# Layer norms scaled by GpSimd, output stores issued by GpSimd, and new ranks, in a two-layer graph network

## The chip, the cores and the metric

The kernel runs on one core of one Trainium2 chip. The metric is device time of one launch in microseconds (us), the median of several runs. The engines of a core are TensorE (PE in the profile, with its weight loads as PEld), VectorE (DVE), ScalarE (ACT), GpSimd (POOL) and SyncE (SP, which here issues transfers). Each engine works through its own queue in order. A change of about 0.2% is the least that a measurement of this kernel can tell from none.

## The reference

Sixteen batches of 1024 nodes with 128 features share one 0/1 adjacency matrix. Two layers follow one another, each with a residual and a layer norm:

```python
def _layernorm(x, axis=-1, eps=1e-5):
    m = jnp.mean(x, axis=axis, keepdims=True)
    v = jnp.var(x, axis=axis, keepdims=True)
    return (x - m) / jnp.sqrt(v + eps)
# layer 0: graph attention
h = x @ others_weight
e = leaky(u1[:, idx1] + u2[:, idx2])        # u1 = h @ a1, u2 = h @ a2
att = softmax(where(adj > 0, e, NEG_BIG), axis=1)
x = _layernorm(x + (att @ h + x @ self_weight))
# layer 1: gated graph network, 5 steps
for _ in range(5):
    m = adj @ h                              # in_matrix = out_matrix = adj, biases as given
    u3 = h @ u3_w.T + u3_b
    z = sigmoid([m, m] @ w3_w.T + w3_b + u3)
    r = sigmoid([m, m] @ w4_w.T + w4_b + u3)
    hv = tanh([m, m] @ w5_w.T + w5_b + r * h @ u5_w.T + u5_b)
    h = (1 - z) * h + z * hv
out = _layernorm(x + h)
```

## The kernel before

**Tiling.** A batch is 1024 nodes by 128 features, worked in two halves `g` (or `e`) of 512 nodes. Batches go in pairs `q = b // 2`. Inside a gated step h is held transposed (`hT`, features on the partitions); the products with the adjacency need it with nodes on the partitions. For these products a value is split in two fp32r parts, by a ScalarE cast (L603) and a VectorE subtraction (L607), into tiles `blk`; the matmuls are those of `product` (L615). For most pairs and steps the two batches' products are combined into seven instead of eight block products, with sums of operand tiles by VectorE (L1061); the first steps of the first pair and the last three steps of the last pair are taken plainly (`PLAIN`).

**A gated step** (`gates`, L1154). For each half: PE multiplies h by u3 (L1170), ScalarE copies it (L1173), PE adds m's part of the r and z gates (L1180), ScalarE takes their tanh (L1183; sigmoids are taken by tanh of the half), VectorE makes r times h (L1190), PE forms the candidate in two matmuls, the second of which reads r's product (L1196, L1197), ScalarE takes its tanh (L1205), and VectorE updates h in three operations (L1208, L1211, L1214).

**From a step to the next** (`leave`, L1228). VectorE transposes h in 32x32 blocks into a tile `T` (L573), SP writes it to DRAM tile `X` in four transfers of 64 KB (`away`, L583) and reads it back with nodes on the partitions into a tile `G` (`back`, L591). In some places PE transposes instead (L565).

**The two layer norms** (`layernorm`, L516). For each half: VectorE's statistics of four 128x128 chunks (`look`, L521, L523), GpSimd's (variance + eps) to the power -1/2 on 128x4 values (`power`, L527 to L537, with a bias -mean times that for the scale that follows), and the scale: four ScalarE activations with scale and bias (`scale`, L542), or, for the very last halves, four VectorE operations that subtract and multiply (`scale_short`, L548). The first norm (`y`) reads what came back from DRAM into tile `F`; for batches 0 and 1 it reads PSUM. Its result goes to tile `y0`, to DRAM tile `yd` by SP (L991), and on to the second layer. The second norm (`o`) works in an `o` tile, of which there are two: SP loads `yd` into it (L1270), VectorE adds h (L1281), statistics, power and scale follow in place, and SP stores it to the output (L1302, 256 KB a half). Odd batches work with the sign of h turned against the even ones (`sign`), which is why `power` has two forms.

**What sets the order.** All operations are added to a `Plan` (L36) with an engine, a length, a rank, what they read and write, and where needed a lag from their end to a reader's start. `Plan.order` runs through these as a list schedule: of what is ready on an engine, the lowest rank goes first, provided that tiles of its kind are free (`"o": (2, ...)` and so on). What comes out is a fixed order for each engine. The numbers in `D` (L303) are added to the rank of a batch and step, `10 * (b // 2) + 4.2 * s`; `LATER` is added for batch 15 in its plain steps; `LATE` is the lag of the loads in `back`; `IDLE` is a number of filler pairs of PE transposes with the worst rank. The planned lengths and lags only order the work: on the chip every engine waits for what its next instruction reads.

Of the kernel before, what the change touches and what calls it, by code (L numbers as in the profile page):

```python
# [13 lines left out]
ALU = mybir.AluOpType  # L14
AX = mybir.AxisListType

P = 128
# [8 lines left out]
LOW, HIGH = -20.0, 100.0  # L26
TINY = 1e-30
PLAIN = {(0, 0), (0, 1), (0, 2), (7, 2), (7, 3), (7, 4)}
LATER = 1
AHEAD = range(4, 12)  # L30
LATE = 3001
TURNED = {(0, 0), (7, 2), (7, 3)}
IDLE = 100

# [103 lines left out]
def kernel(  # L138
# [51 lines left out]
    nc = tc.nc  # L190
    B = x_t.shape[0]
# [26 lines left out]
    def exact(pools):  # L218
# [80 lines left out]
        def sp(*a, **k):  # L299
            plan.add("SP", *a, **k)  # L300


        D = dict(m=-0.2, pu=1.4, u=0.2, pr=0.2, pz=1.4, r=1.7, pv=1.0, z=0.3, hv=0.2, h=0.8, tr=1.2, o=4.2, ln=3.3)  # L303
        D.update(out=4.0, l1=-9, l2=-3, l3=-3, l4=-4, l5=-4, l6=-3.5, l7=0, l8=-2)

        def on_pe(b, what):

            return b < 2 and what in ("y", "b") or b >= B - 3 and what == STEPS - 1 or (b // 2, what) in TURNED
# [8 lines left out]
        def rank0(b):  # L317
            return 10 * (b // 2) - 1 * (1 - b % 2) + -1.0

        def sign(b):  # L320

            return 1 if b % 2 else -1
# [190 lines left out]
            dve(2 * V, 1 + c / 4, t24, reads=[*y, (("tab",), c, 0)], writes=[(("tab",), c, 1)])  # L513


        def layernorm(key, g, rank, after, src, dst, write, sg=1, short=False):  # L516
            stats, mv, rstd = ("stats", *key, g), ("mv", *key, g), ("rstd", *key, g)

            def look():
                for j in range(4):  # L520
                    nc.vector.bn_stats(T(stats)[:, j, :], src(j))  # L521
                for j in range(4):
                    nc.vector.bn_aggr(T(mv)[:, j, :], T(stats)[:, j, :])  # L523

            def power():
                mean, var, r = T(mv)[:, :, 0], T(mv)[:, :, 1], T(rstd)
                nc.gpsimd.tensor_scalar(r[:, 0, :], var, EPS, None, ALU.add)  # L527
                nc.gpsimd.tensor_tensor(r[:, 0, :], r[:, 0, :], mhalf[:, 0:4], ALU.pow)
                if short:
                    if sg < 0:  # L530
                        nc.gpsimd.tensor_scalar(r[:, 0, :], r[:, 0, :], -1.0, None, ALU.mult)
                elif sg > 0:
                    nc.gpsimd.tensor_scalar(r[:, 1, :], mean, -1.0, None, ALU.mult)
                    nc.gpsimd.tensor_tensor(r[:, 1, :], r[:, 1, :], r[:, 0, :], ALU.mult)
                else:
                    nc.gpsimd.tensor_tensor(r[:, 1, :], mean, r[:, 0, :], ALU.mult)
                    nc.gpsimd.tensor_scalar(r[:, 0, :], r[:, 0, :], -1.0, None, ALU.mult)  # L537

            def scale():
                r = T(rstd)  # L540
                for j in range(4):
                    nc.scalar.activation(  # L542
                        dst(j), src(j), AF.Identity, bias=r[:, 1, j : j + 1], scale=r[:, 0, j : j + 1]
                    )

            def scale_short():
                for j in range(4):
                    nc.vector.tensor_scalar(  # L548
                        dst(j), src(j), T(mv)[:, j, 0:1], T(rstd)[:, 0, j : j + 1], ALU.subtract, ALU.mult
                    )  # L550

            after = after if isinstance(after, list) else [after]
            dve(1100, rank, look, reads=after, writes=[(stats, 0), (mv, 0)])
            plan.add("POOL", 2301 if short else 3001, rank, power, reads=[(mv, 0)], writes=[(rstd, 0)])
            if short:
                dve(900, rank, scale_short, reads=[*after, (mv, 0), (rstd, 0)], writes=[write])
            else:
                act(1250, rank, scale, reads=[*after, (mv, 0), (rstd, 0)], writes=[write])
# [66 lines left out]
        def layer0(b):  # L625
# [323 lines left out]
            for g in range(2):  # L949
                rank = rank0(b) + D["l5"]  # L950

                def y(g=g):
                    return T(yT[g])

                t = ("ps", "t", b, "y", g)
                if on_pe(b, "y"):
                    transposes(y, [(yT[g], 0)], t, rank)
                else:
                    k, d, t = (x + (b, "y", g) for x in (("T",), ("D",), ("F",)))
                    turn(k, y, [(yT[g], 0)], rank)  # L960
                    away(k, d, rank)
                    back(d, t, rank)

                def src(j, t=t, flat=on_pe(b, "y")):
                    return T(t)[:, j * P : (j + 1) * P] if flat else chunks(T(t))[:, j]

                def dst(j, g=g, flat=on_pe(b, "y")):
                    c = T(y0[g])[:, j, :]
                    return c if flat else c.rearrange("p (a j) -> p a j", a=4)

                layernorm(("y", b), g, rank0(b) + D["l6"], (t, 0), src, dst, (y0[g], 0), sign(b))

            if not plain(b // 2, 0):

# [253 lines left out]
        def leave(b, s):  # L1228

            rank = rank_of(b, s)  # L1230
            hT = ("hT", b)
            for g in range(2):

                def h(g=g):
                    return T(hT)[:, g * HALF : (g + 1) * HALF]

                k, d = ("T", b, s, g), ("X", b, s + 1, g)
                if s < STEPS - 1 and on_pe(b, s):
                    t = ("ps", "t", b, s, g)
                    transposes(h, [(hT, g)], t, rank + D["tr"])  # L1240
                    split(
                        ("blk", b, "h", s + 1, g),
                        lambda t=t: T(t).rearrange("p (c a j) -> p c a j", c=4, a=4),
                        [(t, 0)],
                        rank_of(b, s + 1),
                    )
                    continue
                if s < STEPS - 1:
                    turn(k, h, [(hT, g)], rank + D["tr"])
                    away(k, d, rank + D["tr"])  # L1250
                    continue

                t = ("ps", "t", b, s, g)
                n = pieces(b, s)
                done = [(hT, g)] if n == 1 else [(hT, g, i) for i in range(n)]
                if on_pe(b, s):
                    for i in range(n):
                        transposes(h, [done[i]], t, rank + D["tr"], range(4 * i // n, 4 * (i + 1) // n), i)
                else:
                    t = ("F", b, s, g)  # L1260
                    turn(k, h, [(hT, g)], rank + D["tr"])
                    away(k, d, rank + D["tr"])
                    back(d, t, rank + D["o"])


                o, yd = ("y0" if b == B - 1 else "o", b, "o", g), ("yd", b, g)
                sp(
                    450,
                    rank + (D["o"] if b < B - 1 else 0),
                    lambda o=o, yd=yd: nc.sync.dma_start(T(o).rearrange("p c d -> p (c d)"), T(yd)),  # L1270
                    reads=[(yd, 0), (hT, g) if b < B - 1 else (("m", b, s, 0), 0)],
                    writes=[(o, "y")],
                    lag=2300,
                )
                for i in range(n):

                    def last(i=i, t=t, o=o, flat=on_pe(b, s)):
                        cs = slice(4 * i // n, 4 * (i + 1) // n)
                        x = T(o)[:, cs, :].rearrange("p c (a j) -> p c a j", a=4)
                        v = T(t).rearrange("p (c a j) -> p c a j", c=4, a=4) if flat else chunks(T(t))  # L1280
                        nc.vector.tensor_tensor(x, v[:, cs], x, ALU.add)  # L1281

                    dve(V / n, rank + D["o"], last, reads=[(t, i), (o, "y")], writes=[(o, "raw", i)])

                def at(j, o=o):
                    return T(o)[:, j, :]

                layernorm(
                    ("o", b),
                    g,  # L1290
                    rank + D["ln"],
                    [(o, "raw", i) for i in range(n)],
                    at,
                    at,
                    (o, 0),
                    sign(b),
                    b == B - 1 or b == B - 2 and g,
                )
                sp(
                    450,  # L1300
                    rank + D["out"],
                    lambda o=o, g=g: nc.sync.dma_start(  # L1302
                        out[b].rearrange("(c p) d -> p c d", p=P)[:, 4 * g : 4 * g + 4, :], T(o)
                    ),
                    reads=[(o, 0)],
                )


        def look_at(i):
# [336 lines left out]
```

## Time and profile before

| what | before |
| --- | --- |
| median of three runs | 1468.24 us (1467.56 to 1468.84) |
| the profiled execution | 1466.94 us, its span 1465.1 us |
| PE busy | 1444.8 us (99%) |
| VectorE busy | 1170.5 us (80%) |
| ScalarE busy | 896.5 us (61%), of it the scales of L542 47.8 for `o`, 46.0 + 6.0 for `y` |
| GpSimd busy | 157.0 us (11%), of it the power itself (L528) 39.9 + 38.3 |
| mean granted TensorE clock | 0.995 |
| transfers issued | all by SP: 568 writes of transposed h, 144 loads `G`, 30 + 30 `o` loads and output stores, among others |

"Busy" is time in which an engine executes; a wait says that the next instruction of an engine had not got what it reads. A line of a group gives the source line, engine, operation, output and inputs, count, then summed busy time, mean ns of one, and the idle time ahead with what ended it. Overlapping instructions of one engine are counted once in its busy time. `SPq` is SP's queue of transfers: a wait there holds every transfer behind it.

### The profile page before, as it was taken

Reading aid. Unit: us, or ns where it says so; the run is one execution under the profiler, and the core shown is the slowest. Engines: PE = TensorE matmul, PEld = TensorE weight load, DVE = VectorE, ACT = ScalarE, POOL = GpSimd, SP = SyncE. Lnnn points to the kernel's source line nnn. Section 1 sums busy time; section 2 is a strip of 40 time slices with the busy share of each in tenths; the row PEclk is TensorE's granted clock in tenths of the full one; section 3 lists DMA queues with packets and bytes.
Section 4 is the critical chain, followed back from the end, with each engine's and each line's share of the span. In section 5 each row is a group of like instructions: output and inputs, shape, how many; then the busy total and the mean of one; then the engine's idle time right before and its main releaser. Section 6 shows DMA issues by size and latency. Waiting matters only on the chain. (4 is left out here: it accounts for less than half of the span.)

```text
span 1465.1 us, 17965 instructions
## 1 busy us (share of the span) xinstructions
PE 1444.8 (99%) x5084; PEld 907.3 (62%) x5084; DVE 1170.5 (80%) x2777; ACT 896.5 (61%) x1790; POOL 157.0 (11%) x260
## 2 busy tenths in 40 slices
PE   9999999999999999999999999999999999999996
PEld 7767656665666566666666665666666666566563
DVE  6777689878888788987888798996889877866435
ACT  5564665667666666576667676556666666654543
POOL 0101100011100210110201110100201102000101
PEclk9999999999999999999999999999999999999998
DMA  8325724464435553455534543455424444223201
GB/s 300 137 68 156 217 72 137 122 188 130 123 101 155 169 145 84 145 146 153 142 103 128 166 130 93 119 149 165 130 75 128 133 133 117 70 65 87 72 0 32
DMA packets 207233, 182.61 MB, mean 125 GB/s; under 512 B 34751, under 2 KB 154262, under 8 KB 207126
## 3 DMA queue, kind: packets, MB, share of 16 engines
q1 hardware_dynamic: 206562, 180.54, 42.4%
q8 instruction: 42, 0.69, 0.2%
q10 hardware_dynamic: 564, 0.85, 0.2%
q14 instruction: 65, 0.53, 0.1%
HBM read 100.92 MB, written 80.39 MB: 124 GB/s over the span
## 5 line engine op out<-in xcount | busy, mean ns | idle before, releaser
L1197 PE MATMUL ps_g_v<-r,u5h 128*128 128x512 f32 x320 | 163.7, 593 | 2.7 <-DVE r L1190 2.7
L1196 PE MATMUL ps_g_v<-m,wm 128*128 128x512 f32 x320 | 163.4, 592 | 0.0
L1180 PE MATMUL ps_g_r<-m,wm 128*128 128x512 f32 x320 | 160.4, 598 | 0.5 <-ACT gz L1173 0.5
L1180 PE MATMUL gz<-m,wm 128*128 128x512 f32 x320 | 158.8, 592 | 0.0
L1208 DVE TENSOR_TENSOR hv<-hv,hT 128x512 f32<-128x512 f32 (+1 forms) x162 | 109.8, 679 | 56.5 <-ACT hv L1205 56.0
L1170 PE MATMUL ps_g_r<-hT,u 128*128 128x512 f32 x320 | 152.8, 592 | 0.0
L615 PE MATMUL ps_acc_a<-tab,blk_s 128*128 128x512 f32 x544 | 146.8, 412 | 0.1
L1183 ACT ACTIVATE r<-ps_g_r,bh 128x512 f32<-128x512 f32 x160 | 109.1, 686 | 57.5 <-PE ps_g_r L1180 54.9
L1190 DVE SCALAR_TENSOR_TENSOR r<-r,hT 128x512 f32<-128x512 f32 x160 | 108.4, 683 | 42.4 <-ACT r L1183 41.8
L615 PE MATMUL ps_acc_po<-adj,blk 128*128 128x512 f32 x512 | 139.0, 420 | 0.0
L1183 ACT ACTIVATE z<-gz,bh 128x512 f32<-128x512 f32 x160 | 109.7, 687 | 28.0 <-PE gz L1180 27.6
L615 PEld LDWEIGHTS ps_acc_a<-tab,blk_s 128*128 128x128 f32 x544 | 100.9, 188 | 33.1 <-issue 8.0
L615 PEld LDWEIGHTS ps_acc_po<-adj,blk 128*128 128x128 f32 x512 | 96.0, 188 | 35.3 <-issue 10.3
L1173 ACT COPY gz<-ps_g_r 128x512 f32<-128x512 f32 x160 | 91.5, 573 | 42.5 <-PE ps_g_r L1170 40.7
L1197 PEld LDWEIGHTS ps_g_v<-r,u5h 128*128 128x128 f32 x320 | 60.4, 189 | 80.1 <-issue 60.2
L1214 DVE SCALAR_TENSOR_TENSOR hT<-hv,hT 128x512 f32<-128x512 f32 (+1 forms) x162 | 108.0, 670 | 1.7
L1211 DVE SCALAR_TENSOR_TENSOR hv<-z,hv 128x512 f32<-128x512 f32 (+1 forms) x162 | 108.1, 670 | 1.5 <-ACT z L1183 0.4
L1180 PEld LDWEIGHTS gz<-m,wm 128*128 128x128 f32 x320 | 60.7, 190 | 74.3 <-issue 73.8
L573 DVE STREAM_TRANSPOSE T<-hT 128x512 f32<-128x512 f32 x142 | 99.0, 700 | 0.2
L615 PE MATMUL ps_acc<-adj,blk_h 128*128 128x512 f32 x384 | 97.6, 407 | 1.2 <-ACT blk_h L603 0.8
L603 ACT CAST blk_s<-G 128x512 fp32r<-128x512 f32 x136 | 82.9, 617 | 22.0 <-DVE G L1061 19.1
L607 DVE TENSOR_TENSOR blk_s<-G,blk_s 128x512 fp32r<-128x512 f32 x136 | 90.7, 678 | 6.8 <-ACT blk_s L603 6.2
(176 smaller groups left out, 2481.5 us busy)
## 6 DMA issues: line engine op xcount, KB each, us to landing
G<-X SPq DMA_DIRECT2D x144, 256.0 KB
X<-T SPq DMA_DIRECT2D x568, 64.0 KB
yd<-y SPq DMA_DIRECT2D x32, 256.0 KB
xt<-in_x_dram SPq DMA_DIRECT2D x15, 512.0 KB
o_o<-yd SPq DMA_DIRECT2D x30, 256.0 KB
out_dram<-o_o SPq DMA_DIRECT2D x30, 256.0 KB
pb<-ud SPq DMA_DIRECT2D x14, 512.0 KB
D_y<-T_y SPq DMA_DIRECT2D x112, 64.0 KB
```

Source lines behind the costliest of these rows:

```text
L573: nc.vector.transpose(T(t).rearrange("p (b c i) -> p b c i", b=4, c=4), turned(src()))
L615: nc.tensor.matmul(T(bank), T(blk)[:, k, c, :], right(c), start=(first and i == 0), stop=(last and i == len(terms) - 1), skip_group_check= ...
L1170: nc.tensor.matmul(T(pr), u3, h(), start=True, stop=True)
L1173: nc.scalar.copy(T(pz), T(pr))
L1180: nc.tensor.matmul(T(p_), wm[:, j, :], T(m), start=False, stop=True, skip_group_check=True)
L1183: nc.scalar.activation(T(t), T(p_), AF.Tanh, bias=bh[:, j : j + 1], scale=0.5 * sg)
L1190: lambda r=r, h=h: nc.vector.scalar_tensor_tensor(T(r), T(r), 1.0, h(), ALU.add, ALU.mult),
L1196: nc.tensor.matmul(T(pv), wm[:, 2, :], T(m), start=True, stop=False)
L1197: nc.tensor.matmul(T(pv), u5h, T(r), start=False, stop=True)
L1208: nc.vector.tensor_tensor(T(hv)[:, w], T(hv)[:, w], h()[:, w], ALU.subtract)
L1211: nc.vector.scalar_tensor_tensor(T(hv)[:, w], T(z)[:, w], 1.0, T(hv)[:, w], ALU.add, ALU.mult)
L1214: nc.vector.scalar_tensor_tensor(h()[:, w], T(hv)[:, w], 0.5, h()[:, w], ALU.mult, ALU.add)
```

## The change

Three things are changed together. The layer norms' scale goes from ScalarE to GpSimd wherever the values lie in SBUF: `y` of batches 2 to 15 and `o` of batches 0 to 13, 56 halves of four operations each. GpSimd subtracts the mean and multiplies by the power, so that `power` no longer needs the bias: odd batches lose two small operations, even ones lose one and do their sign first. The output stores of batches 0 to 13 are issued by GpSimd, with a planned length of 900 and a lag of 2600 ns to the next use of the tile. The last two batches keep the old scales and SP's stores. And `LATER`, `LATE` and seven of the offsets `D` are set anew.

```diff
-LATER = 1
+LATER = 2.5
-LATE = 3001
+LATE = 3801
-        D = dict(m=-0.2, pu=1.4, u=0.2, pr=0.2, pz=1.4, r=1.7, pv=1.0, z=0.3, hv=0.2, h=0.8, tr=1.2, o=4.2, ln=3.3)
-        D.update(out=4.0, l1=-9, l2=-3, l3=-3, l4=-4, l5=-4, l6=-3.5, l7=0, l8=-2)
+        D = dict(m=-0.2, pu=1.4, u=0.4, pr=0.6, pz=1.4, r=1.9, pv=0.6, z=0.7, hv=0.2, h=0.8, tr=1.2, o=4.2, ln=3.3)
+        D.update(out=3.6, l1=-9, l2=-3, l3=-3, l4=-4, l5=-4, l6=-3.5, l7=0, l8=-1)
...
-        def layernorm(key, g, rank, after, src, dst, write, sg=1, short=False):
+        def layernorm(key, g, rank, after, src, dst, write, sg=1, short=False, own=False):
...
-                if short:
+                if short or own:
...
+            def scale_own():
+                for j in range(4):
+                    nc.gpsimd.tensor_scalar(
+                        dst(j), src(j), T(mv)[:, j, 0:1], T(rstd)[:, 0, j : j + 1], ALU.subtract, ALU.mult
+                    )
...
-            if short:
+            if own:
+                plan.add("POOL", 2001, rank, scale_own, reads=[*after, (mv, 0), (rstd, 0)], writes=[write])
+            elif short:
...
-                layernorm(("y", b), g, rank0(b) + D["l6"], (t, 0), src, dst, (y0[g], 0), sign(b))
+                layernorm(("y", b), g, rank0(b) + D["l6"], (t, 0), src, dst, (y0[g], 0), sign(b), own=not on_pe(b, "y"))
...
                     b == B - 1 or b == B - 2 and g,
-                )
-                sp(
-                    450,
-                    rank + D["out"],
-                    lambda o=o, g=g: nc.sync.dma_start(
-                        out[b].rearrange("(c p) d -> p c d", p=P)[:, 4 * g : 4 * g + 4, :], T(o)
-                    ),
-                    reads=[(o, 0)],
-                )
+                    b < B - 2,
+                )
+
+                def out_(o=o, g=g, by=nc.gpsimd if b < B - 2 else nc.sync):
+                    by.dma_start(out[b].rearrange("(c p) d -> p c d", p=P)[:, 4 * g : 4 * g + 4, :], T(o))
+
+                if b < B - 2:
+                    plan.add("POOL", 900, rank + D["out"], out_, reads=[(o, 0)], writes=[((o, "sent"), 0)], lag=2600)
+                else:
+                    sp(450, rank + D["out"], out_, reads=[(o, 0)])
```

## The prediction

> **What bounds the kernel now.** I read the page's busy times first, then the windows, then the waits of TensorE, then the timeline around each wait. The windows come first here (columns: window, its length, then busy us and count of PE, weight loads, VectorE, ScalarE, GpSimd, then granted clock, DMA share, GB/s):
>
> ```profile
> 0.00:100.00 100.00, 98.66 (x512) 72.17 (x513) 70.38 (x241) 59.45 (x153) 9.23 (x25) 1.00 0.52 179
> 100.00:200.00 100.00, 98.25 (x372) 64.18 (x371) 78.94 (x209) 55.95 (x118) 9.88 (x16) 1.00 0.51 151
> 200.00:500.00 300.00, 300.00 (x1032) 188.66 (x1031) 257.28 (x592) 188.85 (x375) 29.19 (x48) 1.00 0.48 138
> 500.00:600.00 100.00, 97.91 (x326) 59.87 (x324) 89.00 (x203) 64.73 (x129) 11.92 (x16) 0.98 0.43 120
> 600.00:1300.00 700.00, 699.92 (x2344) 432.37 (x2343) 585.60 (x1333) 450.20 (x882) 82.07 (x128) 1.00 0.44 125
> 1300.00:1400.00 100.00, 98.45 (x335) 60.59 (x334) 55.45 (x111) 50.68 (x90) 7.92 (x16) 1.00 0.24 71
> ...
> 1450.00:1465.10 15.10, 1.61 (x10) 0.80 (x8) 9.95 (x47) 1.15 (x3) 4.41 (x7) 0.64 0.24 75
> ```
>
> TensorE (PE) is busy 1444.8 of 1465.1 us. All it lacks is 1.3 at the head, 1.75, 2.1, 0.1, 1.55 in mid-stream and 13.5 in the last 15. "Busy" is modelled at its ends, so I also summed the matmuls at the spacing that they show where nothing waits (0.43 us for an fp32 512-column one, 0.23 for fp32r): 1437 us, of which 22 are fillers, and 15 us of gaps: 1.8 at the start, 2.5 at 172-180, 4.1 at 500-510 (of which some 1.7 is a clock of 0.98), 2.1 at 1370-1378, 2.5 before the last transposes at 1453, and scraps; another 11.3 follow the last matmul. The change leaves PE's instructions the same, so **the most that it can win in mid-stream is about 8.5 us**. What PE waited for (us in all, times, longest):
>
> ```profile
> PE ps_t L565 <- DVE hT L1214: 3.3, 2, 2.3
> PE ps_g_v L1197 <- DVE r L1190: 2.7, 2, 2.1
> ...
> PE ps_acc L615 <- ACT blk_h L603: 0.8, 1, 0.8
> PE ps_g_r L1180 <- ACT gz L1173: 0.5, 1, 0.5
> ```
>
> Behind these stand loads, not ScalarE's load of work. At 500 ScalarE's cast waited 3.73 us for `G<-X`, its r tanh and VectorE's r product stood behind it, and PE waited 2.09 us at 504.47; at 178 a cast waited 3.00 for another `G<-X`:
>
> ```profile
> 178.13 0.62 ACT L603 CAST blk_h<-G 128x512 fp32r<-128x512 f32 x1 [3.00 <-DMA G<-X]
> ...
> 500.29 0.62 ACT L603 CAST blk_x<-G 128x512 fp32r<-128x512 f32 x1 [3.73 <-DMA G<-X]
> ```
>
> At 1370 and 1378 it is an `o` load. VectorE's add (L1281) waited for it 7.8 us, and the load stood in SP's queue behind the store of an earlier batch from the same buffer (waits of VectorE, then of SP's queue: us in all, times, longest):
>
> ```profile
> DVE o_o L1281 <- DMA o_o<-yd: 12.3, 4, 7.8
> ...
> SPq L1302 <- ACT o_o L542: 124.2, 21, 70.6
> ...
> SPq L1270 <- DMA out_dram<-o_o: 22.1, 12, 3.0
> ```
>
> So SP's queue loses 124 us waiting for ScalarE's scale and 22 for stores to land. This queue, and not ScalarE (896.5 us, 61%), is where the change can bring something.
>
> **What the Trainium skill says.** "SBUF — State Buffer", section Who interferes with whom: a VectorE instruction with two SBUF inputs and a GpSimd instruction that reads SBUF exclude each other for a whole instruction. The trace agrees for GpSimd: its 128x4 add took 0.50 us at 254.03 while such a VectorE operation ran, and 0.23 where none did; VectorE's two-input operations took 0.68 either way. From the timeline:
>
> ```profile
> 253.79 0.66 DVE L607 TENSOR_TENSOR blk_s<-G,blk_s 128x512 fp32r<-128x512 f32 x1
> ...
> 254.03 0.50 POOL L527 TENSOR_SCALAR rstd_y<-mv_y 128x4 f32<-128x4 f32 x1 [97.33 <-ACT r L1183]
> ```
>
> "DMA: Bandwidth & Descriptors", section Issuing engines are not separate DMA queues: issuing elsewhere saves only sequencer time; GpSimd's path has a first byte at about 1 us against 0.6 (Specifications). No store here goes by GpSimd, so no run shows it yet.
>
> **The change, part by part.** Base: this execution, 1466.94 us (span 1465.1 and 1.84 around it); the median of the runs shown is 1468.24, 1.30 above.
>
> *Scale off ScalarE.* Its groups:
>
> ```profile
> L542 ACT ACTIVATE o_o<-o_o,rstd_o 128x128 f32<-128x128 f32 x116 | 47.8, 485 | 7.4 <-DVE o_o L1281 3.0 <-DMA X<-T 1.5 <-DVE mv_o L523 1.3
> L542 ACT ACTIVATE y<-F_y,rstd_y 128x128 f32<-128x128 f32 x112 | 46.0, 484 | 1.6 <-POOL rstd_y L534 1.6
> ```
>
> Of the 116, 112 go, and all of the second row's. 224 at 0.485 summed 108 us, some 92 without their overlap; ScalarE falls to about 805. PE never waited for L542, and ScalarE waited at the two stalls for a load: worth 0 by itself; it shortens the queue ahead of later r and z tanh's. If this cover is missing, nothing is lost.
>
> *Scale onto GpSimd.* No row has this operation. Below: the tiny operations' 0.23 us plus 124 more elements at the 1.03 cycles of 1.2 GHz ("GPSIMD Engine Reference", 3.1) = 0.34; GpSimd's only 128x128 operations in the trace, a memset of 0.20 and a select of 0.29, agree. Above: 1.8 cycles and a wait for one VectorE operation, 0.23 + 0.19 + 0.3 = 0.72. I take 0.55, an estimate: 2.2 us per half against ScalarE's 1.65, 123 in all. The power step loses two tiny operations of 0.36-0.55 in odd batches and one of some 0.4 in even ones: about 34 us of GpSimd in all, 0.6 per half. So the chain power-scale is as long as before; GpSimd goes from 157 to some 250, plus 28 stores, below 20%. Behind a scale on GpSimd's queue stand only other halves' powers, scales and stores; the scale waits for nothing but its power, whose statistics came from the same tile. In the changed order both powers come first in some batches (o of 3, 11, 12, 13): there the first half's scale waits for the second half's statistics too, which I count at 1-3 us of delay, with the stores below. Of y, the readers are SP's store of y (it waited 57 us in all for ScalarE's scale) and the transposes for the second layer, tens of us of PE work ahead of their use: 0.
>
> *What it does to VectorE.* 0 to 0.34 us for each of 224 = 0 to 76 us on 1170. At most 1.4 us per half, and four at once only if each hits. Cover: between r's product and the PE operation that reads it 98% of the pairs have 1.25 us or more (median 3.2). I take 0.5 us in all; if VectorE really stood 1.4 us in each half, those in the stretch with VectorE at 89.00 of 100 would show.
>
> *Stores by GpSimd.* 28 issues of about 0.4 leave SP (11 us of SP, which is not full), and with them SP's 124 us of waiting on the scale, nearly all of which stood before other loads and writes. The wait isn't gone: the next `o` load (L1270), still on SP, waits until the store has landed, since there are two `o` buffers. Behind a blocked L1270 stand SP's writes of h (L583) and loads of G and F (L591), and behind those ScalarE's casts. Its price: at present store to next load takes 2.4 us (1356.85 to 1359.23, 1361.02 to 1364.40); with 0.4-1 more for the software path, and in pairs where GpSimd runs two powers and two scales before the first store some 2.5 more. Even to odd reload took 7.5-12.6 us and becomes 8-15. In mid-stream the add has slack; before the last pair's plain steps it did not (the 7.8 above).
>
> *Ranks.* LATE puts the loads of G 0.8 us later in the plan, hence further behind their writes on SP: the waits for `X<-T` (70.4 us over 109) shrink, and the loads behind them run earlier. In the new order the add of batch 13 has 28-30 us of PE work between its inputs and its reader, where it had 20-24: I expect the 1370 and 1378 stalls gone (-2.1, I take -1.8). The q=0 load that stalled at 178 has 18.1 us of PE work for it instead of 16.3: gains 1.8, of a stall of about 1.4 with its second part: -1.4. Around 504 the instructions stand differently and the r product has 3 us: -2.2 (the clock's 1.7 stay). Against it: the last steps' u to r distance falls from 1.34 to 0.86 us in two places, 0.2 each, the shortest v product to next split falls from 18.6 to 15.0 (a load chain takes at least 13.5), and fillers are used up by row 169: +0.5 to +2, I take +1.0. LATER 2.5 lets batch 15 trail 14 by half a step; the end's chain of transposes, add, stats, power, scale and store has the same members (batches 14, 15 keep VectorE's scale and SP): 0 +-1.
>
> Sum: -1.4 - 2.2 - 1.8 + 0.5 + 1.0 = -3.9, so 1463.0 for an execution like the profiled one and **1464.3** for the median.
>
> **Rivals.** *No change (chance 0.23):* every reordering of so full a plan makes other loads late; the three stalls leave and as many of 1-2 us come: 1468.2, 1465.3-1471.2. For it: PE at 99%, and causes that are single late loads. Against: the distances above grew at the places that stalled.
>
> *Slower (0.35):* SP is blocked at the `o` load. If the store lands 3-5 us later than the plan supposes (GpSimd held by VectorE's two-input operations, scale above 0.9 us, both scales before both stores), each odd batch's first `o` load holds SP and the G loads behind it. They have 1.5-5 us over the 13.5 us load chain; it decides once SP is held over some 3 us. A third of 28 loads by 1-2 us of PE wait each: 9 x 1.5 = +13, less the 4 gained: 1477, range 1471.2-1485. For it: SP is one queue in order, and the stalls of 1370 were just this. Against: the planner gives the store 2.6 us. VectorE delayed 0.3 us 224 times with a fifth reaching PE gives the same +13.
>
> *The change does not do what it says:* GpSimd so starved that scales pile up: the same as slower, within its 0.35.
>
> **How the numbers follow.** Forecast case 0.42, at 1459-1465.3 (floor: 8.5 off; -0.2% is 1465.3, and 0.2% is about what this kernel's measurement tells from none). Leaving out 0.06 below and 0.14 above gives 1458.5 to 1478; the likeliest case's own range is 1459-1465.3.
>
> **What would show it.** Right: PE busy near 1442-1445 of a span near 1461; no ScalarE wait of 3 us for `G<-X` at 178 and 500; no 7.8 us wait of the add; GpSimd 250-290 busy with scale rows of 0.35-0.7; last matmul to end still about 11. Wrong: scale rows above 0.9 us; SP waiting at the `o` load over 60 us in all; VectorE's r product or h update waiting for GpSimd; new PE waits on casts or on r summing to over 5 us.

## The result, and the profile after

The changed kernel takes 1485.46 us (1483.48 to 1489.29, four runs) against 1467.9 us for the kernel before in the same comparison: a ratio of 1.0124 with a 95% interval of 1.0101 to 1.0147. It is **1.2% slower**, 17.6 us, where 1464.3 us and a small gain were forecast. The range (1458.5 to 1478) does not hold it. The profiled execution took 1483.48 us, its span 1481.7.

First the busy times of the changed kernel's page, then its windows (columns as before: window, length, busy us and count of PE, weight loads, VectorE, ScalarE, GpSimd, then clock, DMA share, GB/s):

```profile
PE 1449.9 (98%) x5084; PEld 907.4 (61%) x5084; DVE 1174.7 (79%) x2777; ACT 816.0 (55%) x1566; POOL 426.4 (29%) x428
```

```profile
100.00:200.00 100.00, 99.11 (x380) 64.22 (x378) 78.06 (x205) 49.89 (x104) 21.39 (x26) 1.00 0.53 153
200.00:500.00 300.00, 296.64 (x1017) 186.46 (x1016) 257.26 (x592) 169.21 (x325) 94.28 (x82) 1.00 0.47 135
500.00:600.00 100.00, 96.07 (x318) 59.38 (x317) 84.37 (x195) 55.99 (x106) 32.76 (x30) 0.98 0.41 114
600.00:1300.00 700.00, 692.43 (x2302) 425.09 (x2301) 583.90 (x1328) 399.74 (x748) 238.43 (x224) 1.00 0.45 126
1300.00:1400.00 100.00, 98.71 (x319) 58.03 (x318) 63.63 (x124) 51.27 (x83) 20.96 (x27) 1.00 0.25 69
```

ScalarE fell to 816 us (805 was expected), VectorE hardly moved, and **GpSimd rose to 426 us where some 250 to 290 were expected**. TensorE now idles 31.75 us of its span (20.3 before), and all of the increase lies in mid-stream: 3.4 us in 200-500 and 7.6 in 600-1300, where it had stood still for next to nothing before, and 1.8 more than before in 500-600. Elsewhere some 1.2 us were won. Its busy time rose by another 5.1 us with the same matmuls. One more stretch at a lower granted clock makes some 1.7 of that (last section); the rest was not followed up, and may lie in the modelled ends of stalled matmuls. Idle and busy time together make the 16.6 us by which the span grew.

The groups of the scale in the changed kernel (count | busy, mean ns of one | idle before):

```profile
L554 POOL TENSOR_SCALAR o_o<-o_o,mv_o,rstd_o 128x128 f32<-128x128 f32 x112 | 140.9, 1267 | 1.6
L554 POOL TENSOR_SCALAR y<-F_y,mv_y,rstd_y 128x128 f32<-128x128 f32 x112 | 139.2, 1252 | 1.9
```

One operation takes **1.26 us, not 0.55**: a half's scale is 5.0 us on GpSimd, against 1.65 on ScalarE and 2.0 in the plan that made the order. Waits of SP's queue, of VectorE and of ScalarE in the changed kernel (us in all, times, longest; the line numbers are mostly 8 higher than before):

```profile
SPq L1278 <- DMA out_dram<-o_o: 100.5, 15, 19.0
...
SPq L999 <- POOL y L554: 53.1, 11, 15.4
...
SPq L999 <- POOL rstd_y L527: 29.9, 8, 9.8
```

```profile
DVE o_o L1289 <- DMA o_o<-yd: 18.0, 7, 5.1
...
DVE T_b L581 <- DMA X<-T: 13.4, 5, 4.9
...
DVE T_b L581 <- POOL y L554: 10.2, 8, 2.4
```

```profile
ACT blk_x L611 <- DMA G<-X: 63.3, 39, 6.8
```

Two of these as they were in the kernel before:

```profile
SPq L991 <- ACT y L542: 57.2, 19, 11.1
```

```profile
ACT blk_x L603 <- DMA G<-X: 27.2, 20, 3.7
```

SP's wait at the `o` load grew from 22.1 to 100.5 us, its waits at the store of y from 57.2 to 83 (for the scale and for the power ahead of it), and ScalarE's wait of its casts of `blk_x` for a load `G<-X` from 27.2 (20 times) to 63.3 (39 times). Followed back from TensorE's larger stalls, two chains appear. One goes through `o`; here it is between 541 and 559 us of the changed kernel (start, duration; engine, line, operation):

```profile
543.26 6.06 POOL L554 TENSOR_SCALAR o_o<-o_o,mv_o,rstd_o 128x128 f32<-128x128 f32 x4
...
549.61 0.86 POOL L1310 DMA_DIRECT2D out_dram<-o_o  x1 [0.29 <-POOL o_o L554]
...
552.51 0.34 SPq L1278 DMA_DIRECT2D o_o<-yd  x1
...
553.28 1.74 SPq L591 DMA_DIRECT2D X<-T  x4
...
555.18 0.34 SPq L599 DMA_DIRECT2D G<-X  x1
```

```profile
558.10 0.62 ACT L611 CAST blk_x<-G 128x512 fp32r<-128x512 f32 x1 [3.85 <-DMA G<-X]
558.63 0.59 ACT L1129 ACTIVATE m<-ps_acc_a 128x512 f32<-128x512 f32 x1
```

```profile
559.27 1.04 PE L623 MATMUL ps_acc_a<-tab,blk_x 128*128 128x512 f32 x2 [2.11 <-ACT m L1129]
```

The scale takes 6.06 us, the store is issued at 549.61 and lands at 552.45, and from 547.5 on SP stands at the next `o` load. Behind it stand the write of h and the load of G; the cast waits 3.85 us for that load, and TensorE 2.11 us for what stood behind the cast on ScalarE. The stalls at 388.8, 1079.2 and 1251.4 lead back to an `o` load in the same way.

The other chain goes through `y`, and was not foreseen. Between 263 and 283 us (timelines of GpSimd, SP, VectorE of the changed kernel):

```profile
263.70 13.36 POOL L554 TENSOR_SCALAR y<-F_y,mv_y,rstd_y 128x128 f32<-128x128 f32 x8
```

```profile
271.82 0.32 SPq L599 DMA_DIRECT2D G<-X  x1
277.08 0.32 SPq L999 DMA_DIRECT2D yd<-y  x1
277.45 0.43 SPq L1009 DMA_DIRECT2D X<-y  x1
277.93 3.89 SPq L591 DMA_DIRECT2D X<-T  x8
```

```profile
281.36 0.71 DVE L581 STREAM_TRANSPOSE T_b<-y 128x512 f32<-128x512 f32 x1 [4.88 <-DMA X<-T]
282.00 0.65 DVE L1137 TENSOR_TENSOR m<-m,ps_acc_c 128x512 f32<-128x512 f32 x1
```

Both halves' scales take 13.4 us. SP has stood at the second half's store of y from 272.1 to 277.08, and the writes of `T` tiles behind it are late. VectorE's transpose of y needs such a tile back and waits 4.88 us (such waits are 13.4 us in all, 0.6 before); its sum of m stands behind it, and TensorE waits for that at 282.7 (1.3 us). The stall at 975 goes back to y's scale in the same way. The one at 850 goes back to it too, but there VectorE's transposes of y themselves wait for the scale (0.73 and 2.17 us).

### The profile page after: what moved, and what is told of

It reads as the page before. It is cut to its first block, busy times and chain, and to the rows that moved or that the text cites. A ratio compares the mean times of both kernels' runs of the same rounds, so it can differ in the third digit from the quotient of the medians.

```text
span 1481.7 us, 17813 instructions
## 1 busy us (share of the span) xinstructions
PE 1449.9 (98%) x5084; PEld 907.4 (61%) x5084; DVE 1174.7 (79%) x2777; ACT 816.0 (55%) x1566; POOL 426.4 (29%) x428
## 5 line engine op out<-in xcount | busy, mean ns | idle before, releaser
L527 POOL TENSOR_SCALAR rstd_y<-mv_y 128x4 f32<-128x4 f32 x32 | 10.7, 333 | 612.8 <-DVE mv_y L523 612.2
L554 POOL TENSOR_SCALAR o_o<-o_o,mv_o,rstd_o 128x128 f32<-128x128 f32 x112 | 140.9, 1267 | 1.6
L554 POOL TENSOR_SCALAR y<-F_y,mv_y,rstd_y 128x128 f32<-128x128 f32 x112 | 139.2, 1252 | 1.9
L527 POOL TENSOR_SCALAR rstd_o<-mv_o 128x4 f32<-128x4 f32 x32 | 17.4, 544 | 419.3 <-DVE mv_o L523 408.9
L623 PEld LDWEIGHTS ps_acc_po<-adj,blk 128*128 128x128 f32 x512 | 95.8, 188 | 35.9 <-issue 11.3
L1188 PEld LDWEIGHTS gz<-m,wm 128*128 128x128 f32 x320 | 60.5, 189 | 73.9 <-issue 73.3
```

The source lines that it names most:

```text
L554: nc.gpsimd.tensor_scalar(dst(j), src(j), T(mv)[:, j, 0:1], T(rstd)[:, 0, j : j + 1], ALU.subtract, ALU.mult)
L623: nc.tensor.matmul(T(bank), T(blk)[:, k, c, :], right(c), start=(first and i == 0), stop=(last and i == len(terms) - 1), skip_group_check= ...
L1188: nc.tensor.matmul(T(p_), wm[:, j, :], T(m), start=False, stop=True, skip_group_check=True)
```

## The experiments

Theory A: the scale takes too long on GpSimd for the order that it is put in, and y and o come late. Rivals: B, the stores through GpSimd hold up SP's loads; C, the new order, ranks included, is worse by itself; later D, y counts as well as o, and E, every new order gives some time by luck. For the last-but-one experiment there are L, a scale is slowed by VectorE's two-input operations, and S, it is slow by itself. All times are medians; ratios are to the kernel before in the same comparison, and are taken over all runs, so that they can differ a little from the quotient of two medians.

**Parts of the change.** The first four kernels take parts of it back. The order is planned anew in each.

```diff
# e1_ranks: only the ranks
-    own=not on_pe(b, "y"))
+    own=False)
-                    b < B - 2,
+                    False,
-    by=nc.gpsimd if b < B - 2 else nc.sync
+    by=nc.sync                          # and planned on SP as before
```

> The changed kernel with only the new ranks: ScalarE scales and SP stores as before. Theory A (a slow scale on GpSimd, 1.26 us an operation in the changed kernel, makes y and o late): within 0.3% of before, 1464 to 1471 us. Theory C (the new order by itself puts work in a worse place): 1476 us or more. Theory B (GpSimd's store path holds SP's queue): as A, 1464 to 1471.

Measured: 1476.48 us, ratio 1.0060 (1.0043 to 1.0077). The ranks by themselves cost 8.8 us, half of the loss by this reading: A missed here, C held. TensorE's larger stalls are two waits at 181.8 and 183.4 (4.0 us together) and one at 898.7 (3.0). This order was made for ScalarE's scales at 1.4 us a half, near the 1.65 that they take, so an order can lose this much without a wrong length for the scale.

```diff
# e2_ranks_stores: ranks and GpSimd's stores, all scales on ScalarE
-    own=not on_pe(b, "y"))
+    own=False)
-                    b < B - 2,
+                    False,
```

> New ranks and GpSimd's stores, all scales on ScalarE. Theory A: 1464 to 1472 us, waits of SP at the o load below 50 us (100.5 in the changed kernel). Theory B: at least half the loss, 1476 us or more, with SP's o-load wait near 100 us.

Measured: 1469.43 us, ratio 1.0011 (1.0002 to 1.0019). B falls: with the stores on GpSimd the kernel is 7 us faster than with the same ranks and SP's stores, though not faster than the kernel before. SP did wait 73.3 us at the `o` load, more than A had said, and it cost TensorE little.

```diff
# e3_o_scale: y's scale back on ScalarE
-    own=not on_pe(b, "y"))
+    own=False)
# e4_y_scale: o's scale back on ScalarE, y's stays
-                    b < B - 2,
+                    False,
```

> The changed kernel with the y scales back on ScalarE; o scales and stores stay on GpSimd. Theory A, by the stalls that lead back to y in the changed trace (282.7, 504.8, 850, 975: some 8 us): 1475 to 1479 us. If only o counts: 1483 to 1487. If only y counts: 1464 to 1471.

> The changed kernel with the o scales back on ScalarE; y scales and o stores stay on GpSimd. Theory A, by the stalls that lead back to the o load (388.8, 559.3, 1079, 1251: some 7 us): 1475 to 1479 us. If only y counts: 1483 to 1487. If only o counts: 1464 to 1471.

Measured: with o's scale on GpSimd and y's on ScalarE 1485.97 us, ratio 1.0121 (1.0104 to 1.0138); the other way 1467.99 us, ratio 1.0000 (0.9991 to 1.0009). Read alone this says that all of the loss is o's and y's scale is free. The next runs show that this reading is too simple.

**The scale's length in an order that stays.** To keep every engine's order and change only what the scale takes, its operations are left out, while the plan still counts them.

```diff
# e5_o_left: o goes out unscaled
             def scale_own():
-                for j in range(4):
+                for j in range(4 if key[0] == "y" else 0):
# e6_o_half: half of o goes out unscaled
+                for j in range(4 if key[0] == "y" else 2):
```

> The changed kernel in its own order on every engine, with the four GpSimd scale operations of o left out (o goes out unscaled). Theory A (the o scale takes too long on GpSimd, 4 to 7 us a half where the order was made for 2.0): 1464 to 1471 us. Theory C (the order that came out with o's scale on GpSimd is bad by itself): 1478 us or more. Theory D (y's scale on GpSimd matters too): 1472 to 1477.

> The changed kernel in its own order, with two of the four GpSimd scale operations of each o half left out. The o scale then takes 2 to 3.5 us, near the 2.0 of the plan. Theory A: less than 40% of the loss stays, below 1475 us; if the loss is linear in the length of the scale, about half of what leaving out all four gives back, some 1476. Theory C: 1478 us or more.

Measured: 1476.51 us (ratio 1.0043, 1.0021 to 1.0064) without any of o's operations and 1475.58 (1.0048, 1.0029 to 1.0067) without half of them. So some 9 to 10 us of the loss are the time that o's scale takes above some 2.5 us a half, since leaving out the second half of it gives nothing more. Some 7 to 8 us stay without any scale of o (the intervals leave about 3 us either way): it is not o alone. In e5 the stalls at 283.95, 288, 848 and 972 are those that led back to y, its largest, 3.4 us at 1149.9, leads back to a late store of y as well, and SP waits 68.1 us for the scale at y's store (53.1 in the change). That speaks for D; no run leaves y's scale out of this order, so what of the 8 us is y's and what the ranks' is not shown.

**The planned length.** The instructions stay those of the changed kernel; the plan is told another length for the scale, and only the order changes.

```diff
# e9 1001, e10 3501, e7 5001, e15 6501 in place of 2001
-                plan.add("POOL", 2001, rank, scale_own, ...
+                plan.add("POOL", 5001, rank, scale_own, ...
# e7 also (it orders nothing: no operation reads what this lag is put on)
-    lag=2600
+    lag=3000
```

> The changed kernel with the scale planned at 5.0 us in place of 2.0 and the store's lag at 3.0 us, so the order is made for the length that it has. Theory A in the form that the order was made for a wrong length: 1464 to 1472 us. If the long chain through two o tiles is itself what costs, whatever the order: 1478 us or more.

> The changed kernel with the scale planned at 1.0 us in place of 2.0, further from the 5.0 that it takes; the instructions are the same, only their order changes. Theory A (the loss comes from an order made for a wrong length): more than the changed kernel, 1486 us or over. Theory E (any new order gives some time between 1464 and 1486 by luck): anywhere, no trend over 1.0, 2.0, 3.5, 5.0 us.

> The changed kernel with the scale planned at 3.5 us. Theory A: between the changed kernel and the one planned at 5.0 us, 1467 to 1479. Theory E: no trend.

> The changed kernel with the scale planned at 6.5 us, more than the mean of 5.0 and near the longest that it takes. Theory A: within 4 us of the one planned at 5.0, 1461 to 1469. Theory E (luck of the order): anywhere to 1486.

Measured:

| planned length of a half's scale | time, us | ratio to before (95%) |
| --- | --- | --- |
| 1.0 us (e9) | 1491.59 | 1.0157 (1.0140 to 1.0174) |
| 2.0 us (the change) | 1485.46 | 1.0124 (1.0101 to 1.0147) |
| 3.5 us (e10) | 1468.24 | 0.9995 (0.9984 to 1.0005) |
| 5.0 us (e7; it takes 5.0) | 1464.81 | 0.9971 (0.9961 to 0.9981) |
| 6.5 us (e15) | 1464.77 | 0.9975 (0.9967 to 0.9983) |

**The time follows the planned length, and comes to rest where the plan knows what the operation takes.** Of the five orders, none breaks the trend, which luck (E) would hardly do. Luck isn't nothing, as e1 shows with its 8.8 us; it is the trend over 26.8 us that carries this, not any one of the orders. The same two moves and ranks that lose 1.2% gain 0.3% on the kernel before when the order is made for the right length. The scale itself is not faster in e7:

```profile
L554 POOL TENSOR_SCALAR y<-F_y,mv_y,rstd_y 128x128 f32<-128x128 f32 x112 | 138.7, 1248 | 1.9
L554 POOL TENSOR_SCALAR o_o<-o_o,mv_o,rstd_o 128x128 f32<-128x128 f32 x112 | 132.8, 1193 | 2.3
```

What has gone are the waits behind it (SP's queue, VectorE and ScalarE of e7), and with them the stalls (windows of e7):

```profile
SPq L1278 <- DMA out_dram<-o_o: 49.7, 11, 10.8
```

```profile
DVE o_o L1289 <- DMA o_o<-yd: 4.2, 3, 2.5
...
DVE T_b L581 <- POOL y L554: 0.5, 1, 0.5
```

```profile
ACT blk_x L611 <- DMA G<-X: 12.7, 10, 2.7
```

```profile
100.00:200.00 100.00, 96.89 (x375) 64.33 (x374) 71.97 (x192) 45.59 (x96) 21.63 (x26) 0.98 0.51 153
200.00:500.00 300.00, 300.00 (x1013) 187.06 (x1012) 264.52 (x603) 174.48 (x334) 90.97 (x82) 1.00 0.47 133
500.00:600.00 100.00, 99.87 (x348) 62.90 (x347) 89.54 (x203) 60.19 (x117) 33.65 (x30) 1.00 0.42 120
600.00:1300.00 700.00, 700.00 (x2342) 431.71 (x2340) 590.15 (x1340) 405.33 (x756) 230.75 (x224) 1.00 0.45 128
1300.00:1400.00 100.00, 100.00 (x334) 60.31 (x333) 57.52 (x114) 48.27 (x79) 23.13 (x30) 1.00 0.23 66
```

VectorE's wait for a `T` tile's write, 13.4 us in the change, is not among e7's waits at all. SP still waits 50 us at `o` loads, but what stands behind them now comes in time. In every one of these windows from 200 on TensorE idles less than in the change.

Which of the two lengths counts:

```diff
# e11_true_y
-                plan.add("POOL", 2001, ...
+                plan.add("POOL", 5001 if key[0] == "y" else 2001, ...
# e12_true_o: the same with "o", and the store's lag at 3000
```

> The changed kernel with only y's scale planned at 5.0 us, o's at 2.0 as in the change. If o's wrong length is what costs (the o scale back on ScalarE gave 1468, the y scale back 1486): 1480 us or more. If both count alike: 1472 to 1478. If y's: below 1470.

> The changed kernel with only o's scale planned at 5.0 us (and its store's lag at 3.0), y's at 2.0 as in the change. If o's wrong length is what costs: 1464 to 1470 us. If both count alike: 1472 to 1478. If y's: 1480 or more.

Measured: 1474.58 us (1.0044, 1.0030 to 1.0058) with y's length true and 1468.48 us (1.0002, 0.9987 to 1.0017) with o's. Each takes away more than half of the 20.7 us between the change and e7 (10.9 and 17.0), so both count and they do not add up. A late half may do harm mainly where the queue is full already; that is a guess, and as these are two more orders, the split is rough. This goes against the reading of e3 and e4 that y is free; why e3, which frees GpSimd of y's scale, gains nothing stays open.

**Taking the wait off SP.**

```diff
# e8_o_load_by_gpsimd
-                    lambda o=o, yd=yd: nc.sync.dma_start(...
+                    lambda o=o, yd=yd, by=nc.gpsimd if b < B - 2 else nc.sync: by.dma_start(...
```

> The changed kernel with the o loads of batches 0 to 13 issued by GpSimd as well, so that SP no longer stands at them; nothing else moves. If the loss comes from what stands behind the o load on SP (loads of G, writes of T): 1466 to 1474 us. If it comes from the late add of o on VectorE, and what stands behind that: 1481 us or more.

Measured: 1505.66 us, ratio 1.0242 (1.0211 to 1.0273), 20 us slower still. The wait did not go away, it moved to GpSimd, and what stands behind it there is later scales and powers; VectorE's wait for the `o` load rose from 18.0 to 34.4 us:

```profile
POOL o_o L1278 <- DMA out_dram<-o_o: 38.0, 14, 3.5
```

So it does not tell how the loss in the change divides between SP's queue and the late add.

**The operation by itself.** GpSimd and VectorE operations are appended after the last layer norm of the kernel before.

```diff
# e13_op_alone, after the plan's last operation
+            own(8, A_)                                  # two values per partition, 128x128
+            8 x nc.gpsimd.tensor_scalar(O[:, 0:P], A_[:, 0:P], 1.0, 2.0, ALU.subtract, ALU.mult)
+            8 x nc.gpsimd.tensor_scalar(O[:, 0:P], A_[:, 0:P], 1.0, None, ALU.subtract)
+            own(4, A_, HALF)                            # 128x512
+            for kind in (two-input add, stream transpose, one-input add of a constant):
+                13 x own(1, ...)  beside  24 x that VectorE operation, 128x512
```

> The kernel before with GpSimd operations appended after the last layer norm (its time is longer by them and says nothing): first alone on the chip's GpSimd, 8 scales of 128x128 with two values per partition, 8 with two constants, 8 with one operation, 4 of 128x512; then 13 scales beside a stream of VectorE additions with two inputs in SBUF, 13 beside 32x32 transposes, 13 beside one-input additions of a constant. Theory L (each scale is slowed by VectorE's two-input operations, not slow for its own sake only): 0.78 us alone, 1.3 to 2.4 beside two-input additions, 0.78 to 0.85 beside transposes. Theory S (it is slow by itself, and what looks like a lock is chance): 0.78 to 0.9 beside all three.

Measured, in the timeline of GpSimd (L1398 the scale, L1404 two constants, L1406 one operation):

```profile
1463.80 7.05 POOL L1398 TENSOR_SCALAR m_bench<-m_bench,bias 128x128 f32<-128x128 f32 x8 [2.65 <-DVE m_bench L1401]
1470.94 5.72 POOL L1404 TENSOR_SCALAR m_bench<-m_bench 128x128 f32<-128x128 f32 x8
1476.74 4.81 POOL L1406 TENSOR_SCALAR m_bench<-m_bench 128x128 f32<-128x128 f32 x8
1481.65 8.60 POOL L1398 TENSOR_SCALAR m_bench<-m_bench,bias 128x512 f32<-128x512 f32 x4
...
1492.46 13.77 POOL L1398 TENSOR_SCALAR m_bench<-m_bench,bias 128x128 f32<-128x128 f32 x12
...
1511.12 10.60 POOL L1398 TENSOR_SCALAR m_bench<-m_bench,bias 128x128 f32<-128x128 f32 x12
...
1530.13 12.37 POOL L1398 TENSOR_SCALAR m_bench<-m_bench,bias 128x128 f32<-128x128 f32 x12
```

Alone a scale takes 0.79 us (8 in 7.05, with 0.1 between two), with constants 0.64, with one operation 0.53, and over 512 columns 2.07. Beside VectorE's two-input additions it takes 0.79 and 1.32 in turn, beside its transposes 0.79, beside its one-input additions of a constant 0.95. Theory L holds: **0.79 is the operation's own, the rest of the 1.26 is waiting for VectorE.** In the changed kernel the shortest is 0.78, the median 1.09 and the longest 2.35. Its trace says the same: the 36 of the 224 scales that overlap no two-input operation of VectorE took 0.78 to 0.82, and the 82 that share 1 us or more with such operations took 1.83 on average.

**The ranks of before.**

```diff
# e14_old_ranks_true: the change planned at 5001 and 3000, with
-LATER = 2.5
+LATER = 1
-LATE = 3801
+LATE = 3001          # and D of the kernel before
```

> Both moves (scales and stores on GpSimd), the scale planned at 5.0 us, with LATER, LATE and the offsets of the kernel before. If the new ranks bring what the 5.0 us kernel gained on before: 1467 to 1476 us. If the moves do: 1461 to 1466.

Measured: 1465.60 us, ratio 0.9982 (0.9974 to 0.9990). The gain is the moves' with a true length, though which of the two moves brings it was not tried; the intervals of the old ranks (e14) and the new ones (e7) overlap. **e7, e14 and e15 are faster than both kernels**, by 2.6 to 3.7 us than the kernel before.

## Why the prediction was wrong

- **What bounds the kernel.** Right: TensorE is at its floor, and the single late loads that cost TensorE could be won back. In e7 TensorE's busy time is 99.87 of 100 in 500-600 and 100.00 in 1300-1400 (97.91 and 98.45 before), which are the gains counted for 504 and 1370-1378. The stall at 178 did not go: 96.89 in 100-200, where 98.25 was. In the change itself it was the other way round: 100-200 came to 99.11, while 1.8 us were lost at 504.8 and 1.3 at 1393.9. That e7's 1464.81 lies beside the forecast of 1464.3 is luck, since the forecast took its gain from the ranks. (The prediction's account of the span, 1437 of matmuls, 15 of gaps and 11.3 at the end, falls 1.8 us short of the 1465.1; no term of the forecast rests on it.)
- **"Scale onto GpSimd", the step that failed.** 0.55 us was taken, with 0.72 as upper end, from operations on 4 columns and a price by element; the operation has 0.79 as its least and takes 1.26 on average. All terms were too small: the slope (512 columns against 128 give 3.3 ns a column, where 0.9 to 1.5 ns had been used), the fixed part (0.37 us by the same two lengths, where 0.23 was used), and the wait for VectorE, set at 0.3 us at the most but 0.47 on average. In "GPSIMD Engine Reference", section 3.1, of the Trainium skill the 1.8 cycles behind the upper end are the best case of a tight loop, so they bounded nothing from above. "So the chain power-scale is as long as before" fell with it: the scale is 5.0 us, not 2.2, and the small operations saved in the power are the 0.6 that was counted.
- **The planned length was accepted as about right.** The prediction let the order stand as made, at 2.0 us planned against 2.2 estimated. The price thus entered twice: as a longer chain, and as an order that puts loads and writes on SP in front of each other for a shorter one. e7 and e9 show that the second is what costs most: at equal instructions 26.8 us lie between a plan of 1.0 and one of 5.0.
- **"Of y ... 0."** Wrong. The readers were looked at, and they have slack, but not what stands behind y's store on SP's queue: writes of `T` tiles, and so VectorE's next transpose (4.88 us at 281). With y's length true 10.9 us come back.
- **"Stores by GpSimd."** Right in the mechanism: the wait is not gone, it moved to the `o` load, from 22.1 to 100.5 us. A store takes 0.84 us of GpSimd and 2.9 from issue to landing (the median of 28; 2.84 at 549.61). Of the prediction's two pairs of a store by SP and the next load, the first is 2.4 us apart and the second 3.4, not 2.4, so the 0.4 that was estimated for GpSimd's path holds against the first only. Two more readings were wrong. Of the 124 us that SP waited for ScalarE's scale, 70.6 were one wait, from 1379 to 1450 us, with nothing but the last stores of the output behind it; it stays in the change, at 57.7. And "the planner gives the store 2.6 us" does not hold, nor does the change's lag of 2600 ns to the next use of the tile: no operation reads the `(o, "sent")` on which that lag is put, and `Plan.order` frees a tile at the end of its last user's length, so the plan lets the next `o` load go 0.9 us after the store begins, about 2 us before it lands. That holds for every run here with GpSimd's stores, and e7 still shows 49.7 us of waiting at that load.
- **"What it does to VectorE", 0.5 us.** Nothing speaks against it, though its cost to TensorE was not measured by itself: VectorE's busy time rose by 4.2 us in 1170, and in e13 one addition in three was longer by 0.13 us (0.69 to 0.82).
- **The rival "slower"** had the mechanism of the `o` load, though not that of y, its sign that a scale above 0.9 us decides, and SP's `o` wait above 60 us, all of which came in; it had 1477 us (13 of waits less 4 gained), up to 1485, and a chance of 0.35, where 1485.46 came. The range cut it off at 1478 because the chance was given to the forecast, whose weakest number was a price with no row. Of that rival's other half (VectorE delayed) the busy times show next to nothing.
- **The ranks.** The claim that they win 4 us net by more distance at three stalls is true for e7 only in two of three; e1 shows the same ranks losing 8.8 us with ScalarE's scales, and e14 that the old ranks do as well with the moves. With the old ranks too TensorE is busy for 100.00 of 100 us in 500-600 and 99.72 in 1300-1400, so it was not the new ranks that won those two stalls back.

## What to carry to other kernels

A list schedule is only as good as the lengths it is given. When an operation moves to another engine, measure it there among its neighbours and give the plan that number; 3 us too little for 56 steps cost 1.4% here, with the engine itself busy 29% of the time. Right lengths alone do not make a good order, as e1 shows. Look also for what the plan doesn't know at all, here the landing of a store. For a step that waits on an in-order transfer queue, look at what stands behind it in the queue, not only at its own readers.

## What the runs showed of the hardware that was not expected

- GpSimd's scale with two values per partition costs 0.79 us for 128x128 and 2.07 for 128x512, with two constants 0.64 (e13); ScalarE's took 0.485 and VectorE's 0.334 in the kernel before.
- "SBUF — State Buffer", section Who interferes with whom, in the Trainium skill says that a VectorE instruction with two SBUF inputs contends with a GpSimd instruction that reads SBUF, and that `tensor_scalar` on VectorE can too, in its two-port mode. e13 agrees: 1.32 us beside two-input additions in every second scale, 0.95 beside one-input additions of a constant, 0.79 beside transposes. The cost falls mainly on GpSimd: a scale was up to 0.53 us longer, a VectorE operation 0.13 at most (every third two-input addition, 0.69 to 0.82; every second one-input addition, 0.43 to 0.56), so in e13 VectorE never waited for a whole scale, as the prediction's wording of that section would have it.
- After some stalls TensorE goes on at half pace, and the traces tell which. In each of 16 traces (all but e13's), once the start is over, the changes of the granted clock lie whole multiples of 3.41 us apart, on a grid that is fixed for the run. In the changed kernel the clock falls to 0.50 at 559.50 and 975.93, for one step of the grid each, which costs some 1.7 us a step (windows, columns as above; the second reaches past the end of its step at 979.34):

```profile
960.00:974.00 14.00, 12.62 (x47) 8.33 (x46) 8.93 (x22) 4.52 (x9) 7.46 (x5) 1.00 0.39 122
976.00:980.00 4.00, 4.00 (x10) 2.49 (x9) 3.37 (x10) 3.06 (x11) 0.00 (x0) 0.58 0.68 172
```

  Laid over TensorE's idle time, the grid tells the stalls apart. Each of the 43 steps in which TensorE stood still for 1.85 us or more was followed by a step at 0.50. Of the steps at full clock with less than 1.7 us none was, and of the seven between these two figures two were. So in these runs it counts whether about half of one step is idle, and not how long a stall is by itself. The stalls of 2.1, 2.1 and 2.4 us at 504 (before), 559 and 975 (after) each fell into one step and were followed by it. In e8 two stalls of 2.85 and 3.25 us, which the grid cut into 1.09 + 1.77 and 1.51 + 1.74, were not.
